# A two-layer kernel (selective scan, then attention): the planner's costs for DMAs, and the queue and the room of the first attention's loads

## The chip, the cores and the metric

The kernel runs on one core of one Trainium2 chip. The metric is the time of one execution on the device, in microseconds. Before the change it is 4532.04 us, the median of three runs (4529.59 to 4533.02).

## The reference

The input `x` is (2, 256, 64, 64) in float32: two images, 256 channels, 4096 positions. Two layers are added to it in turn.

```python
# layer 0: group norm, then a selective-scan block and an MLP
yn = layer_norm(group_norm(x)) * gamma + beta          # over the 256 channels, at each position
xm, z = split(yn @ W_in.T)                              # 512 channels each
u = silu(causal_conv4(xm) + conv_b)
proj = u @ W_xp.T                                       # 16 for dt, 16 for B, 16 for C
dt = softplus(proj[:, :16] @ W_dt.T + b_dt)
h = exp(dt * A) * h + (dt * u) * B                      # for each position, 512 channels x 16 states
y = sum_n(h * C) + u * D
y2 = (y * silu(z)) @ W_out.T + yn
x = x + gelu(y2 @ W1.T + b1) @ W2.T + b2 + y2
# layer 1: group norm, then attention with 8 heads of 32 over the 4096 positions
q, k, v = split(group_norm(x) @ qkv_w.T + qkv_b)
x = x + softmax(q.T @ k / sqrt(32)) @ v.T
```

## The kernel before

Positions are cut into tiles of 512, eight for each image. The kernel has three stages: `mamba_stage` (layer 0 for both images, 16 tiles), then `attention_block` for image 0 and again for image 1. A last check of the softmax sums chooses whether a slow general attention has to run; it does not here.

**The scan.** A tile has 32 steps: four blocks of 128 channels, four groups of four states, two halves. A step multiplies on GpSimd or VectorE (`dbu`, line 809), scans on VectorE (line 814), keeps the last state with a copy on ScalarE (line 817) and multiplies by C on GpSimd (line 820). The decay exponentials are ScalarE's (line 803). The time steps `dt` and `dt * u` go through DRAM so that they can come back replicated over partitions: stores at line 588, loads `dt_rep` and `dtu_rep` at line 767, two of each at the start of a block of channels. Rows of B and C come back the same way (line 779).

**Around it.** `front` prepares the next tile: it loads `yn` (line 481), normalises it (line 479), projects and convolves, and computes `dt`. `back` finishes a tile: the output product, the MLP with eight GELUs into the buffer `hid` (line 646), two long sums over `hid` (line 657), the addition to the loaded `x_back` (line 667), the statistics for the second group norm (line 668) and the store (line 671). From tile 8 on, `qkv` projects one tile of image 0 for the first attention: it loads the weights (line 686) and the tile (line 687) into `hid`, normalises (line 692), makes queries and keys in two halves (lines 705 and 709), stores them (line 714), and does the same for values (lines 741 and 734). `hid` has one buffer, which `back` and `qkv` take in turns.

**The order of work.** None of this is issued as written. Every piece is a task in `Plan`, with an engine, a due step, a cost in microseconds, and for a DMA a time `lands` from its issue being done to its landing. `Plan.order` runs a list schedule in these costs: each engine takes the ready task with the earliest due step, none that is due more than 24 steps behind the oldest open one. A DMA task occupies the planned SP for its cost, and its readers become ready after cost and `lands`. The result is the program order of each engine. On the chip each engine takes its instructions in that order and waits where one is not ready, so a task that was planned too early holds up what stands behind it. All DMAs are issued by SP's queue.

Due steps are written by hand. `qkv(0, t)` is due `QKV` = 20 steps into a tile:

```python
qkv(0, t, (i + 1) * STEPS + QKV)
```

**Room.** Each stage opens pools in on-chip memory, one after the other from the same base, and gives them back at its end. `mamba_stage` has the pool `l0w` (weights and small tables, 51 KB for each partition) and behind it `l0s` (all buffers of the scan, `hid` and `x_back` among them). `attention_block` lays its own pools over the same room, in the order in which they are opened: weights and values (`l1w`: `b_qkv`, `ones`, `v`), queries (`l1p2`), keys (`l1k`), exponentials (`l1e`, `l1c`), and after the loads the result buffers (`l1p1`, `l1p3`) and a key buffer (`l1kq`).

**The attentions.** `attention_block` works on steps of 128 keys by 512 queries for four heads: logits on TensorE (line 1086), exponentials on ScalarE (line 1099), products with the values on TensorE (line 1120), sums on VectorE and GpSimd. For image 0 (`prepared`) queries, keys and values lie in DRAM already, and `load_prepared` brings the first query tile (4 DMAs, line 910), the eight key tiles (2 DMAs each, line 907) and the values (line 1042). For image 1 `prepare` makes them first, which takes about 105 us with the loads at lines 968 and 975.

Of the kernel before, what the change touches and what calls it, by code (L numbers as in the profile page):

```python
# [19 lines left out]
P = 128  # L20
# [81 lines left out]
class Plan:  # L102
# [4 lines left out]

    HANDOVER = 0.2
# [20 lines left out]
    def add(self, engine, due, cost, emit, reads=(), writes=(), tables=(), lands=0.0):  # L129


        task = Plan.Task()
        task.engine, task.due, task.cost, task.emit = engine, due, cost, emit
        task.tables, task.lands, task.at = tables, lands, len(self.tasks)
        deps = set()
        reads, writes = list(self.keys(reads)), list(self.keys(writes))
        for key in reads:
            deps.add(self.writer.get(key))
        for key in writes:
            deps.add(self.writer.get(key))  # L140
            deps.update(self.readers.get(key, ()))
        for key in reads:
            self.readers.setdefault(key, []).append(task)
        for key in writes:
            self.writer[key], self.readers[key] = task, []
        deps -= {None, task}
        task.deps, task.behind = len(deps), []
        task.ready, task.start = 0.0, None
        for dep in deps:
            dep.behind.append(task)  # L150
        task.bufs = list({id(b): b for b, _ in reads + writes}.values())
        for buf in task.bufs:
# [92 lines left out]
QKV = 20  # L245
# [3 lines left out]
def mamba_stage(ctx, tc, xs, stats_out, consts, w, outs, scratch):  # L249
# [220 lines left out]
    def front(i):  # L470
# [10 lines left out]
        add("SP", due - 46, 0.8, lambda: nc.sync.dma_start(yn.tile, image_tile(xs[b], t)), [], [yn], lands=4.0)  # L481
# [58 lines left out]
        add("SP", due - 12, 0.8, store_bc, [bc], [d.bc], lands=2.0)  # L540
# [26 lines left out]
    def softplus(d, k, due):  # L567
# [28 lines left out]
        add("SP", due + 3.5, 0.8, lambda: store(d.dt[k], dt, "dt_dram"), [dt], [d.dt[k]], lands=2.0)  # L596
        add("POOL", due + 3.5, 1.27, lambda: nc.gpsimd.tensor_mul(lw.tile, dt.tile, d.u[k].tile), [dt, d.u[k]], [lw])
        add("SP", due + 4, 0.8, lambda: store(d.dtu[k], lw, "dtu_dram"), [lw], [d.dtu[k]], lands=2.0)
# [12 lines left out]
    def back(i):  # L611
# [26 lines left out]
        add("SP", due + 6, 0.8, lambda: nc.sync.dma_start(xt.tile, image_tile(xs[b], t)), [], [xt], lands=4.0)  # L638
# [33 lines left out]
        add("SP", due + 29, 0.8, store, [xt], [stored[b * NT + t]], lands=3.0)  # L672

    def qkv(b, t, due):
# [19 lines left out]
        add("SP", due, 1.6, load, [stored[b * NT + t]], [hid], lands=6.0)  # L694
        for k in range(KC):
            add("ACT", due + 2, 0.75, lambda k=k: norm(k), [hid[3 + k], scales_buf[(IMAGES + b) * KC + k]], [hid[3 + k]])
        for n, (i, m) in enumerate(((1, 0), (1, 1), (0, 0), (0, 1))):
# [24 lines left out]
            add("SP", at + 1.5, 0.8, store, halves, [], lands=3.0)  # L722
        for j in range(0, T // P, 2):
# [18 lines left out]
            add("SP", at + 1, 1.6, store, [hid[7]], [], lands=3.0)  # L742
# [17 lines left out]
    def load_rep(g, name, src, ring_):  # L760
# [8 lines left out]
        add("SP", g - 7, 0.8, load, [src], [rep], lands=4.5)  # L769
        return rep  # L770

    def load_row(g, ring_, at):
# [8 lines left out]
        add("SP", g - 5, 0.8, load, [tiles[i].bc], [row], lands=4.0)  # L781
# [117 lines left out]
def load_stack(nc, dst, src, which):  # L899

    src = src.rearrange("s c h t -> s c (h t)")
    dst = dst.rearrange("p h t -> p (h t)").bitcast(F32)
    for i in range(2):
        if which:
            nc.sync.dma_start(dst[2 * i * D : 2 * (i + 1) * D, :], src.rearrange("s c x -> (s c) x"))
        else:
            for j in range(2):
                nc.sync.dma_start(dst[(2 * i + j) * D : (2 * i + j + 1) * D, :], src[i])  # L910
# [3 lines left out]
def attention_block(ctx, tc, b, stats, consts, w, out, scratch, range_t, prepared):  # L914
# [15 lines left out]
    wp = ctx.enter_context(tc.tile_pool(name=f"l1w{b}", bufs=1))  # L930
# [3 lines left out]


# [6 lines left out]
    p2 = ctx.enter_context(tc.tile_pool(name=f"l1p2{b}", bufs=2))  # L942
    kp = ctx.enter_context(tc.tile_pool(name=f"l1k{b}", bufs=NT))
    ep = ctx.enter_context(tc.tile_pool(name=f"l1e{b}", bufs=5))
    ec = ctx.enter_context(tc.tile_pool(name=f"l1c{b}", bufs=2))
# [3 lines left out]
    def load_keys(g, t):  # L949
# [3 lines left out]
        load_stack(nc, k, scratch.qk[b * KG + g, 1, t], 1)  # L953

    def load_queries(i):
        if i < KG * NT:
            g, t = divmod(i, NT)
            q = queries[i] = p2.tile([P, 4, T], F32R, name="q")
            load_stack(nc, q, scratch.qk[b * KG + g, 0, t], 0)
# [79 lines left out]
    def load_prepared():  # L1039
        def load_values(g, t):  # L1040
            cs = bass.ts(t, T // P)
            nc.sync.dma_start(v[:, cs, g * P : (g + 1) * P], scratch.v[b * KG + g, :, cs, :])

        with tc.manual_schedule():
            load_queries(0)
            for t in range(NT):
# [195 lines left out]
def attention_any_range(ctx, tc, consts, w, out, scratch):  # L1242
# [20 lines left out]
    with tc.For_i(0, groups, 1) as g:  # L1263
        k = p1.tile([P, NT, 4, T], F32R, name="g_k")
        for t in range(NT):
            load_stack(nc, k[:, t], scratch.qk[bass.ds(g, 1), 1, t].rearrange("o s c h t -> (o s) c h t"), 1)
# [4 lines left out]
        with tc.For_i(0, NT, 1) as t:  # L1271
            q = p1.tile([P, 4, T], F32R, name="g_q")
            load_stack(nc, q, scratch.qk[bass.ds(g, 1), 0, bass.ds(t, 1)].rearrange("o n s c h t -> (o n s) c h t"), 0)
# [120 lines left out]
```

## Time and profile before

| | |
|---|---|
| runs | 4529.59, 4532.04, 4533.02 us |
| profiled execution | 4532.59 us |
| its span, first to last instruction | 4530.8 us |
| scan | 0 to about 2121 us |
| first attention | about 2121 to 3277 us |
| second attention, with its preparation | about 3277 to 4524 us |
| busy over the span: PE, DVE, ACT, POOL | 4248.6, 3931.0, 3762.3, 3821.2 us |
| DMA engines, mean busy share | 28% |

A profile is one execution. Engines are PE (TensorE, with PEld its weight loads), DVE (VectorE), ACT (ScalarE), POOL (GpSimd) and SP, which issues DMAs and is never counted as busy. L820 is line 820 of the kernel. A name such as `h<-h,c` gives what an instruction writes and reads. A wait names the engine and line that ended it. GpSimd and VectorE set the pace of the scan, TensorE that of the attentions (1070.95 us busy of the 1090 us from 2260 on).

### The profile page before, as it was taken

The page shows a single profiled execution, that of the slowest core. Times are in us where ns is not written, and L with a number is a line of the kernel's source. Part 1 is how long each engine was busy: PE and PEld are TensorE (multiplying, and loading weights), DVE is VectorE, ACT ScalarE, POOL GpSimd, SP SyncE. Part 2 cuts the span into 40 slices and gives each one's busy share as a digit, 9 for nine tenths or more (in the row PEclk, how much of TensorE's full clock was granted, in tenths as well). Part 3 has the DMA queues.
Part 4 walks back from the last instruction along what each step waited for, and adds up shares of the span by engine and source line. Part 5 has one row for each costly group of instructions (what it writes and reads, how often), then busy time and mean ns, then how long its engine had stood idle before and what let it go on. Part 6 is the DMA issues. An engine that isn't in the chain of part 4 may idle for free. (4 is left out here: it accounts for less than half of the span.)

```text
span 4530.8 us, 53988 instructions
## 1 busy us (share of the span) xinstructions
PE 4248.6 (94%) x18530; PEld 1638.8 (36%) x18530; DVE 3931.0 (87%) x3316; ACT 3762.3 (83%) x4836; POOL 3821.2 (84%) x2251
## 2 busy tenths in 40 slices
PE   5799989999899999988999999999899999999998
PEld 2233333333333333333333333333343333333333
DVE  4999989999999899994889889898848898898988
ACT  4788888888788888883999999999739999999997
POOL 2999999999999999994888888888708888888887
PEclk8899999999999999999999999999999999999999
DMA  5233333333443344444311040110091100401100
GB/s 191 96 118 114 108 111 121 126 126 126 143 153 124 127 131 135 153 156 106 88 26 26 20 100 17 26 29 20 20 267 40 45 24 22 101 17 26 28 20 8
DMA packets 172938, 389.24 MB, mean 86 GB/s; under 512 B 24048, under 2 KB 50416, under 8 KB 164464
## 3 DMA queue, kind: packets, MB, share of 16 engines
q1 hardware_dynamic: 172656, 385.73, 28.0%
q8 instruction: 147, 2.41, 0.2%
q14 instruction: 135, 1.11, 0.1%
HBM read 292.34 MB, written 93.32 MB: 85 GB/s over the span
## 5 line engine op out<-in xcount | busy, mean ns | idle before, releaser
L1112 DVE TENSOR_REDUCE chunk<-chunk 128x1024 f32<-128x4096 f32 x288 | 1269.9, 4409 | 226.7 <-ACT chunk L1099 226.7
L1099 ACT ACTIVATE chunk<-s 128x1024 f32<-128x1024 f32 x992 | 1116.7, 1126 | 181.2 <-PE s L1086 146.9
L1153 POOL TENSOR_TENSOR acc_p<-acc_p,e 128x1024 f32<-128x1024 f32 x480 | 1153.0, 2402 | 135.2 <-ACT e L1099 114.1
L1086 PE MATMUL s<-q,k 128*128 128x512 f32 x4096 | 1225.6, 421 | 17.5 <-DMA v<-v_dram 14.8
L820 POOL TENSOR_TENSOR h<-h,c 128x1024 f32<-128x1024 f32 x512 | 1206.5, 2368 | 38.4 <-ACT state L817 27.8
L1120 PE MATMUL po<-chunk,v 128*32 128x512 f32 x3968 | 1114.6, 640 | 0.0
L1120 PE MATMUL po<-e,v 128*32 128x512 f32 x4224 | 1079.0, 605 | 0.0
L1099 ACT ACTIVATE e<-s 128x1024 f32<-128x1024 f32 x1056 | 1069.5, 1016 | 7.4 <-PE s L1086 7.0
L1086 PEld LDWEIGHTS s<-q,k 128*128 128x128 f32 x4096 | 689.8, 188 | 1021.5 <-issue 926.4
L803 ACT ACTIVATE da<-dt_rep,neg_a 128x512 f32<-128x512 f32 x1024 | 690.5, 701 | 118.6 <-DVE h L814 87.7
L1151 POOL TENSOR_TENSOR acc_p<-acc_p,e 128x512 f32<-128x512 f32 x480 | 631.2, 1315 | 161.4 <-ACT e L1099 138.6
L814 DVE TENSOR_TENSOR_SCAN h<-da,state,dbu 128x512 f32<-128x512 f32 x512 | 650.3, 1273 | 52.0 <-POOL dbu L809 45.9
L814 DVE TENSOR_TENSOR_SCAN h<-da,state,bn 128x512 f32<-128x512 f32 x512 | 647.4, 1265 | 12.4 <-POOL dt L595 0.5
L809 POOL TENSOR_TENSOR dbu<-dtu_rep,b 128x512 f32<-128x512 f32 x384 | 486.8, 1279 | 30.8 <-DMA dtu_rep<-dtu_dram 27.9
L234 ACT ACT_TABLE_LOAD x338 | 433.7, 1283 | 6.8 <-PEq L1384 0.7
L425 PE MATMUL bn<-proj,pick 112*128 112x512 f32 x512 | 309.2, 617 | 111.3 <-DVE h L814 111.1
L846 PE MATMUL y<-h,sum 128*32 128x512 f32 x2048 | 358.8, 638 | 24.4 <-POOL h L820 24.0
L809 DVE TENSOR_TENSOR bn<-dtu_rep,bn 128x512 f32<-128x512 f32 x512 | 349.1, 682 | 30.6 <-PE bn L425 16.2
L1150 DVE TENSOR_TENSOR acc<-acc,e 128x512 f32<-128x512 f32 x448 | 309.8, 691 | 24.3 <-ACT e L1099 13.8
L1120 PEld LDWEIGHTS po<-chunk,v 128*32 128x32 f32 x3968 | 142.9, 108 | 360.7 <-issue 349.6
L425 PE MATMUL mm<-yn,w_in 128*128 128x512 f32 x512 | 250.4, 615 | 12.3 <-ACT yn L514 9.3
L425 PE MATMUL mm<-xm,taps 128*128 128x512 f32 x512 | 237.1, 606 | 11.1 <-POOL xm L561 8.7
(135 smaller groups left out, 4068.4 us busy)
## 6 DMA issues: line engine op xcount, KB each, us to landing
dt_rep<-dt_dram SPq DMA_DIRECT2D x128, 512.0 KB, 5.0
dtu_rep<-dtu_dram SPq DMA_DIRECT2D x128, 512.0 KB, 5.5
q<-qk_dram SPq DMA_DIRECT2D x128, 256.0 KB, 4.8
k<-qk_dram SPq DMA_DIRECT2D x64, 512.0 KB, 8.1
b<-bc_dram SPq DMA_DIRECT2D x64, 256.0 KB, 3.1
c<-bc_dram SPq DMA_DIRECT2D x64, 256.0 KB, 4.6
dt_dram<-dt SPq DMA_DIRECT2D x64, 256.0 KB, 2.1
dtu_dram<-lw SPq DMA_DIRECT2D x64, 256.0 KB, 3.4
```

The source lines that it names most:

```text
L234: self.nc.scalar.preload_act_table_set(self.TABLES[task.table])
L425: nc.tensor.matmul(out, lhsT=lhsT, rhs=rhs, start=(i == 0), stop=(i == len(pairs) - 1))
L803: nc.scalar.activation(da[j].tile, dt.tile[:, j, :], AF.Exp, scale=scale)
L809: engine.tensor_mul(out.tile, dtu.tile[:, j, :], rows.tile)
L814: nc.vector.tensor_tensor_scan(h.tile[:, j, :], da[j].tile, dbu.tile, initial, ALU.mult, ALU.add)
L820: nc.gpsimd.tensor_tensor(h.tile, h.tile, rows_c.tile.unsqueeze(1).to_broadcast([P, 2, T]), ALU.mult)
L1086: nc.tensor.matmul(ps[:, j, :], lhsT=keys[i // NT, kt][:, h, kj : kj + P], rhs=queries[i][:, h, :], start=True, stop=True)
L1099: nc.scalar.activation(e, todo[s].s[half], AF.Exp, scale=SCALE)
L1112: nc.vector.tensor_reduce(out, terms, AX.XY, ALU.add)
L1120: nc.tensor.matmul(tiles[i].po[h * D : (h + 1) * D, :], lhsT=v[:, c, g * P + h * D : g * P + (h + 1) * D], rhs=todo[s].e[h // 2][:, h % 2, :],
L1151: nc.gpsimd.tensor_add(acc_p[:, 1, :], acc_p[:, 1, :], eb[:, 1, :])
L1153: nc.gpsimd.tensor_add(acc_p, acc_p, eb)
```

## The change

There are two parts.

The planner counts DMAs by their bytes: a load or store of 512 KB holds the planned SP for 1.7 us and lands 3.3 us later, one of 256 KB holds it for about 0.9. In the steps before 32 the cost is at most 0.8. `QKV` goes from 20 to 16. In `qkv` the weights come in two loads of half the size, planned as tasks of their own behind the tile's load.

The first attention's pools are opened in another order, so that exponentials lie over the weights' pool, and queries, result buffers, keys and values over the scan's. Its first query tile, first key tile and first values are issued by ScalarE's queue, as its first instructions behind the scan's; the others stay on SP's.

```diff
     def add(self, engine, due, cost, emit, reads=(), writes=(), tables=(), lands=0.0):
+        if engine == "SP" and due < 32:
+            cost = min(cost, 0.8)
...
-QKV = 20
+QKV = 16
...
-        add("SP", due - 46, 0.8, lambda: nc.sync.dma_start(yn.tile, image_tile(xs[b], t)), [], [yn], lands=4.0)
+        add("SP", due - 46, 1.7, lambda: nc.sync.dma_start(yn.tile, image_tile(xs[b], t)), [], [yn], lands=3.3)
...
-        add("SP", due - 12, 0.8, store_bc, [bc], [d.bc], lands=2.0)
+        add("SP", due - 12, 0.4, store_bc, [bc], [d.bc], lands=1.6)
...
-        add("SP", due + 3.5, 0.8, lambda: store(d.dt[k], dt, "dt_dram"), [dt], [d.dt[k]], lands=2.0)
+        add("SP", due + 3.5, 0.9, lambda: store(d.dt[k], dt, "dt_dram"), [dt], [d.dt[k]], lands=2.0)
...
-        add("SP", due + 6, 0.8, lambda: nc.sync.dma_start(xt.tile, image_tile(xs[b], t)), [], [xt], lands=4.0)
+        add("SP", due + 6, 1.7, lambda: nc.sync.dma_start(xt.tile, image_tile(xs[b], t)), [], [xt], lands=3.3)
...
-        add("SP", due + 29, 0.8, store, [xt], [stored[b * NT + t]], lands=3.0)
+        add("SP", due + 29, 1.7, store, [xt], [stored[b * NT + t]], lands=3.3)
...
+        def load_weights(c):
+            nc.sync.dma_start(weights(c, 0, 3 * C), w["qkv_wT"][c * P : (c + 1) * P, :])
+
         def load():
-            nc.sync.dma_start(flat(0, 3).rearrange("p (k f) -> p k f", k=KC), w["qkv_wT"].rearrange("(k p) f -> p k f", p=P))
             nc.sync.dma_start(hid.tile[:, 3:5, :], image_tile(outs[b], t))
...
-        add("SP", due, 1.6, load, [stored[b * NT + t]], [hid], lands=6.0)
+        add("SP", due, 1.7, load, [stored[b * NT + t]], [hid], lands=3.3)
+        for c in range(KC):
+            w_parts = [hid[0]] if c == 0 else [hid[1], hid[2]]
+            add("SP", due + 1 + c, 1.3, lambda c=c: load_weights(c), [], w_parts, lands=3.0)
...
-            add("SP", at + 1.5, 0.8, store, halves, [], lands=3.0)
+            add("SP", at + 1.5, 1.7, store, halves, [], lands=3.3)
...
-            add("SP", at + 1, 1.6, store, [hid[7]], [], lands=3.0)
+            add("SP", at + 1, 1.0, store, [hid[7]], [], lands=2.5)
...
-        add("SP", g - 7, 0.8, load, [src], [rep], lands=4.5)
+        add("SP", g - 7, 1.7, load, [src], [rep], lands=3.3)
...
-        add("SP", g - 5, 0.8, load, [tiles[i].bc], [row], lands=4.0)
+        add("SP", g - 5, 0.9, load, [tiles[i].bc], [row], lands=3.0)
...
-    wp = ctx.enter_context(tc.tile_pool(name=f"l1w{b}", bufs=1))
+    def pool(name, bufs):
+        return ctx.enter_context(tc.tile_pool(name=f"l1{name}{b}", bufs=bufs))
+
+    def late_pools():
+        return pool("p1", 1), pool("p3", 2)
...
+    ec, ep, p2 = pool("c", 2), pool("e", 5), pool("p2", 2)
+    if prepared:
+        p1, p3 = late_pools()
+    kp, wp = pool("k", NT), pool("w", 1)
...
-    def load_keys(g, t):
+    def load_keys(g, t, queue=nc.sync):
...
-        load_stack(nc, k, scratch.qk[b * KG + g, 1, t], 1)
+        load_stack(queue, k, scratch.qk[b * KG + g, 1, t], 1)
...
         with tc.manual_schedule():
-            load_queries(0)
-            for t in range(NT):
+            load_queries(0, nc.scalar)
+            load_keys(0, 0, nc.scalar)
+            load_values(0, 0, nc.scalar)
+            for t in range(1, NT):
                 load_keys(0, t)
                 load_values(0, t)
...
-    load_prepared() if prepared else prepare()
-
-    p1 = ctx.enter_context(tc.tile_pool(name=f"l1p1{b}", bufs=1))
-    p3 = ctx.enter_context(tc.tile_pool(name=f"l1p3{b}", bufs=2))
-    kq = ctx.enter_context(tc.tile_pool(name=f"l1kq{b}", bufs=1))
+    if prepared:
+        load_prepared()
+    else:
+        prepare()
+        p1, p3 = late_pools()
+    kq = pool("kq", 1)
```

The store of `dtu_dram` changes as that of `dt_dram` does. `load_stack`, `load_queries` and `load_values` take the queue in the same way as `load_keys`.

More of the change, by code (lines that the diff above doesn't have):

```diff
@@ L595, in softplus @@
         add("POOL", due + 3, 1.27, lambda: nc.gpsimd.tensor_add(dt.tile, dt.tile, lw.tile), [lw], [dt])
-        add("SP", due + 3.5, 0.8, lambda: store(d.dt[k], dt, "dt_dram"), [dt], [d.dt[k]], lands=2.0)
+        add("SP", due + 3.5, 0.9, lambda: store(d.dt[k], dt, "dt_dram"), [dt], [d.dt[k]], lands=2.0)
         add("POOL", due + 3.5, 1.27, lambda: nc.gpsimd.tensor_mul(lw.tile, dt.tile, d.u[k].tile), [dt, d.u[k]], [lw])
-        add("SP", due + 4, 0.8, lambda: store(d.dtu[k], lw, "dtu_dram"), [lw], [d.dtu[k]], lands=2.0)
+        add("SP", due + 4, 0.9, lambda: store(d.dtu[k], lw, "dtu_dram"), [lw], [d.dtu[k]], lands=2.0)
     def gate(d, k, due):
@@ L896, in image, with load_stack @@
         return self.x[b * KG : (b + 1) * KG].rearrange("g c t -> (g c) t")
-def load_stack(nc, dst, src, which):
+def load_stack(queue, dst, src, which):
     src = src.rearrange("s c h t -> s c (h t)")
@@ L906, in load_stack @@
         if which:
-            nc.sync.dma_start(dst[2 * i * D : 2 * (i + 1) * D, :], src.rearrange("s c x -> (s c) x"))
+            queue.dma_start(dst[2 * i * D : 2 * (i + 1) * D, :], src.rearrange("s c x -> (s c) x"))
         else:
             for j in range(2):
-                nc.sync.dma_start(dst[(2 * i + j) * D : (2 * i + j + 1) * D, :], src[i])
+                queue.dma_start(dst[(2 * i + j) * D : (2 * i + j + 1) * D, :], src[i])
 @with_exitstack
@@ L941, in attention_block, with load_queries @@
     v = wp.tile([P, NC, C], F32, name="v")
[L942 to L945, printed above, removed]
     keys = {}
     queries = {}
-    def load_keys(g, t):
+    def load_keys(g, t, queue=nc.sync):
         k = keys[g, t] = (kq if g and t == 0 else kp).tile([P, 4, T], F32R, name="k")
-        load_stack(nc, k, scratch.qk[b * KG + g, 1, t], 1)
-    def load_queries(i):
+        load_stack(queue, k, scratch.qk[b * KG + g, 1, t], 1)
+    def load_queries(i, queue=nc.sync):
         if i < KG * NT:
@@ L958, in load_queries @@
             q = queries[i] = p2.tile([P, 4, T], F32R, name="q")
-            load_stack(nc, q, scratch.qk[b * KG + g, 0, t], 0)
+            load_stack(queue, q, scratch.qk[b * KG + g, 0, t], 0)
     def s_tile():
@@ L1039, in load_prepared, with load_values @@
     def load_prepared():
-        def load_values(g, t):
+        def load_values(g, t, queue=nc.sync):
             cs = bass.ts(t, T // P)
-            nc.sync.dma_start(v[:, cs, g * P : (g + 1) * P], scratch.v[b * KG + g, :, cs, :])
+            queue.dma_start(v[:, cs, g * P : (g + 1) * P], scratch.v[b * KG + g, :, cs, :])
         with tc.manual_schedule():
-            load_queries(0)
-            for t in range(NT):
+            load_queries(0, nc.scalar)
+            load_keys(0, 0, nc.scalar)
+            load_values(0, 0, nc.scalar)
+            for t in range(1, NT):
                 load_keys(0, t)
@@ L1265, in attention_any_range @@
         for t in range(NT):
-            load_stack(nc, k[:, t], scratch.qk[bass.ds(g, 1), 1, t].rearrange("o s c h t -> (o s) c h t"), 1)
+            load_stack(nc.sync, k[:, t], scratch.qk[bass.ds(g, 1), 1, t].rearrange("o s c h t -> (o s) c h t"), 1)
         v = p1.tile([P, NC, P], F32, name="g_v")
@@ L1272, in attention_any_range @@
             q = p1.tile([P, 4, T], F32R, name="g_q")
-            load_stack(nc, q, scratch.qk[bass.ds(g, 1), 0, bass.ds(t, 1)].rearrange("o n s c h t -> (o n s) c h t"), 0)
+            load_stack(nc.sync, q, scratch.qk[bass.ds(g, 1), 0, bass.ds(t, 1)].rearrange("o n s c h t -> (o n s) c h t"), 0)
             o = p1.tile([P, T], F32, name="g_o")
```

## The prediction

> **What bounds the kernel now.** I read the page's table of slices first (two even stretches and dips near slices 20 and 30), then busy time by stretch of one scan tile, then the waits of GpSimd and ScalarE in the second half of the scan, the DMA issues, and the timeline where the scan hands over to the first attention. The page's chain of waits ends inside the last 20 us and says nothing of the change.
>
> Busy time in stretches of 123 us (length, then PE, PEld, DVE, ACT, POOL, granted clock, DMA share, GB/s):
>
> ```profile
> 725.00:848.00 123.00, 113.48 (x348) 42.82 (x347) 115.24 (x126) 103.73 (x171) 122.00 (x78) 0.99 0.35 116
> 848.00:971.00 123.00, 114.18 (x347) 43.14 (x346) 115.52 (x127) 103.12 (x171) 122.00 (x80) 0.97 0.35 118
> ...
> 1340.00:1463.00 123.00, 113.93 (x351) 44.43 (x349) 110.92 (x123) 104.00 (x171) 114.43 (x74) 0.97 0.41 135
> 1463.00:1586.00 123.00, 113.14 (x359) 44.71 (x359) 110.23 (x121) 101.07 (x166) 114.16 (x73) 0.99 0.42 140
> ```
>
> In the first image GpSimd works 122.0 of 123 us: nothing is to be won there. In the second, where the projections for the first attention are woven in, it works 114. The last gate product of each tile (line 856 in the timeline) shows the same: tiles 5 to 7 end 120.8 us apart, tiles 8 to 14 end 124.8, 129.4, 128.5, 128.8, 128.1, 126.2 and 125.9 apart. Against 120.8 that is 46 us, the most that a better order could bring. The waits between 1000 and 2090 us (sum, times, longest), first GpSimd's, then ScalarE's:
>
> ```profile
> POOL h L820 <- ACT state L817: 23.3, 25, 3.1
> POOL dbu L809 <- DMA dtu_rep<-dtu_dram: 16.4, 10, 2.5
> ```
>
> ```profile
> ACT hid L705 <- DMA qk_dram<-hid: 24.3, 11, 4.0
> ACT yn L479 <- DMA yn<-in_x: 21.5, 6, 4.9
> ACT da L803 <- DMA dt_rep<-dt_dram: 18.7, 14, 2.8
> ```
>
> The reader is to see two things: GpSimd waits 16.4 us for a transfer itself, and 23.3 us for ScalarE, which in turn sits 64.5 us in its queue before work whose transfer comes later than the planner thought. What transfers take (KB each, median us from issue to landing):
>
> ```profile
> dt_rep<-dt_dram SPq DMA_DIRECT2D x128, 512.0 KB, 5.0
> dtu_rep<-dtu_dram SPq DMA_DIRECT2D x128, 512.0 KB, 5.5
> ...
> qk_dram<-hid SPq DMA_DIRECT2D x32, 512.0 KB, 4.6
> ```
>
> **Part 1, the planner's costs and QKV.** No instruction of the scan is added but one DMA per `qkv` (its weights in two loads instead of one, 8 more issues at 0.39 us each, the row of line 686, on SP, which is idle most of the time: nothing on the path). What changes is the order on each queue. A store of the two halves is now planned to land after 1.7 + 3.3 = 5.0 us, before 0.8 + 3.0 = 3.8, measured 4.6. The four replicated loads that open a block of channels were planned to land at 5.3, 6.1, 6.9 and 7.7 us and are now at 5.0, 6.7, 8.4 and 10.1 (each holds SP 1.7 instead of 0.8); measured 5.0 and 5.5 in the median and up to 9.0. So consumers of late transfers move back in their queues, behind work that is ready. The load of `yn` goes from 4.8 to 5.0, which leaves its 21.5 us. So 24.3 + 18.7 = 43.0 of ScalarE's 64.5 us can go, two thirds; two thirds of GpSimd's 23.3 is 15.5. I take half of that (7.8) and half of the 16.4 (8.2), because a list schedule fills only part of what it now sees: -16. Bounds: all of 16.4 + 23.3, -40; no gain, and a loss through `qkv`, +24, priced under the rivals. Where the stall goes, VectorE is late next: 110 to 112 busy of 123 in those stretches, with 10 us to spare.
>
> The Trainium skill speaks against these costs: "DMA: Bandwidth & Descriptors", section "Anatomy of one DMA — SWDGE (gpsimd) path", fits a transfer as 2.0 us plus its bytes over 436 GB/s, for GpSimd's queue, which for 512 KB makes an estimate of 3.2 us. By it the planner would now be 1.8 us too slow with every such load and part 1 would bring nothing; the rows of 5.0 and 5.5 us on this queue are what I go by.
>
> The start (due below 32) keeps 0.8, with landings 0.7 to 1.2 us earlier than planned before; GpSimd waits 7.4 us there for `dtu_rep`. Either sign, 3 us at most: 0. QKV = 16 raises the rank of the projections by four steps. It does not start them sooner, as `hid` has one buffer: the load at 1320.0 us comes right behind the last matmul that reads `hid`. At the end of the scan it may move one projection (matmuls at 2085.09, 1.88 us) out from between the two output products of the last tile: -1 (0 to -1.9).
>
> **Part 2, the hand-over to the first attention.** The timeline (start, duration, instruction, idle time before):
>
> ```profile
> 2104.36 0.69 ACT L646 ACTIVATE hid<-mm,b 128x512 f32<-128x512 f32 x1 [1.03 <-PE mm L425]
> ...
> 2119.82 0.75 DVE L667 SCALAR_TENSOR_TENSOR x_back<-mm,b,x_back 128x512 f32<-128x512 f32 x1 [6.25 <-PE mm L657]
> ...
> 2120.59 0.37 SPq L671 DMA_DIRECT2D x_dram<-x_back  x1
> ...
> 2120.69 0.12 POOL L940 MEMSET ones<- 128x32 f32 x1 [40.17 <-DVE x_back L667]
> ...
> 2121.53 2.40 SPq L910 DMA_DIRECT2D q<-qk_dram  x4
> 2124.11 1.17 SPq L907 DMA_DIRECT2D k<-qk_dram  x2
> ...
> 2134.61 0.77 PE L1086 MATMUL s<-q,k 128*128 128x512 f32 x1 [14.83 <-DMA v<-v_dram]
> ```
>
> ScalarE is free from 2105.05 us, SP is held by the last store until 2120.59, and TensorE waits 14.83 us for the first loads. If ScalarE's queue could issue at 2105, these would be gone. But look at the memset of `ones`. It is the second small tile of the attention's first pool and lies over the input's statistics, the first tile of the weights' pool, last used long ago. Yet it waits until 2120.6 for the addition that reads `b_2`, the last use of anything in that pool. A new pool's room is free when the whole old pool is. The scan's buffers are one pool too, and `x_back` is in it: its last store is issued at 2120.59 and lands at 2123.45. The waiting instructions of ScalarE, VectorE and GpSimd ahead of their first work over that pool end at 2123.47 to 2123.52, ScalarE's for `chunk`, which lies nowhere near `x_back`. After the change `q`, `k`, `v` lie over the scan's pool alone, so I expect the first load on ScalarE's queue at 2123.5, not 2105, and 2.0 us later than SP's at 2121.53. Its seven issues (2.40 + 1.17 + 0.59 = 4.2 us on SP) hold up only the exponentials, which need their data anyway. The next issues are now on two queues at once: SP follows its small `b_qkv` (3.4 us to land) with the second keys, while ScalarE still has queries and first keys on the way. In the old order q and the first k took 12.7 us from first issue to landing (2121.53 to 2134.20). The DMA engines were 0.89 busy in these 14.8 us with one queue, so a second one only takes turns. From about 2127.5 some 7.2 us of the first loads' transfer time (k lands every 2.4 us) are left; shared in equal turns they take 14.4. So the first matmul comes 2.0 us later with no sharing and 9.2 with full sharing: I take +5, near the middle, since some of SP's loads wait for a landing before they are issued. Low end, if the loads do start at 2105: -13 (rival 1).
>
> On two queues the same page, section "Issuing engines are not separate DMA queues", says that they run on the same 16 engines and that only the issuing time is saved; by it the hand-over would cost the full 9 us, and no run so far has a second queue to show it.
>
> **Part 3, the second hand-over.** The new layout puts the second attention's preparation over the first one's values and not over its result buffers. Its weights' load was issued at 3279.54, once the last result's store (3277.22) had landed at 3279.34; it can now follow the `b_qkv` load, at 3278.1: -1.4 (0 to -1.9). The attentions themselves keep their instructions.
>
> **Sum.** The profiled execution took 4532.59 us (span 4530.8 and 1.8 around it), 0.5 over the median of the runs. 4532.6 - 16 + 5 - 1.4 - 1 = 4519. The forecast's own range is 4496 to 4530.
>
> **Rivals.**
> 1. The loads do start behind the GELU. For it: ScalarE is idle for 30.89 us there. Against: the 40.17 us of `ones`. They would be landed by 2119, the first matmul moves from 2134.61 to 2120.6, and the second keys on SP, issued near 2121.6, cost back about 1: -13 instead of +5, 4501.
> 2. Slower: the `hid` buffer sets the pace. In `qkv` the weights are now planned behind the image's load, since that writes all of `hid`: 5.0 + 1.3 + 1.3 + 3.0 = 10.6 us before the first projection may be planned, 7.6 before. On the chip SP's order follows this. `hid` is held in turn by one projection round and one MLP, a round every 128 us, so 3.0 us in each of 8 rounds would add 24 with no gain to set against: 4532.6 + 24 + 5 - 2.4 = 4559. For it: the first GELU of tile 9 comes 50 us after that tile's end (33 in tile 0). Against: 27 us lie between the last projection (1368) and that GELU, room enough to hide 3. It decides if the time from the load of `qkv` to its first normalisation, 10.1 us now, grows by 3 and the GELUs move with it.
> 3. GpSimd's waits only change their names: its idle time stays near 59.6 us between 1000 and 2090, as VectorE and TensorE (93%) are nearly as full. 4532.6 + 5 - 2.4 = 4535.
>
> **Chances.** Forecast 0.48, rival 1 0.10, rival 2 0.25, rival 3 0.17. A measurement of this kernel tells about 0.2% (9 us) from no change. Faster by more: 0.40 of the forecast and rival 1, 0.50. Within: 0.08 of the forecast and 0.13 of rival 3, 0.21. Slower: rival 2 and the rest of rival 3, 0.29. The range runs from 4494 to 4556: below rival 1's time, and nearly to rival 2's.
>
> **What will show it.** Right: tiles 8 to 14 end near 126 us apart; ScalarE's waits for `qk_dram<-hid` and `dt_rep` halve; the first `q` is issued about 3 us after the last `x_back` addition, and the first matmul of the logits follows 16 to 23 us after that addition (14.0 now). Wrong: a `q` issued before that addition (rival 1), or GpSimd's waits in the second half as large as before under other names.

## The result, and the profile after

The changed kernel takes 4530.25 us in the median of 12 runs (4521.69 to 4533.14), the kernel before 4531.79 beside it (12 runs, 4528.81 to 4536.74). The ratio is 0.9996, with a 95% interval of 0.9988 to 1.0003: no difference that this measurement can tell.

The profiled execution of the changed kernel is the fastest of its twelve (4521.69 us, span 4519.9). Against the profile of before it is 10.9 us shorter, where the medians differ by 1.5. So two profiles alone mislead here, and the phases below are read from several.

First the stall lists, as in the prediction: waits between 1000 and 2070 us (the scan now ends at 2060), sum, times, longest; ScalarE, then GpSimd.

```profile
ACT da L812 <- DVE h L823: 59.9, 59, 2.9
ACT state L826 <- DVE h L823: 52.4, 80, 3.9
ACT hid L714 <- PE mm L429: 20.8, 16, 5.6
ACT da L812 <- DMA dt_rep<-dt_dram: 9.5, 8, 2.6
...
ACT yn L483 <- DMA yn<-in_x: 2.7, 2, 1.9
ACT hid L698 <- DMA hid<-x_dram: 1.6, 2, 1.4
```

```profile
POOL h L829 <- ACT state L826: 17.9, 22, 2.7
POOL dbu L818 <- DMA dtu_rep<-dtu_dram: 7.5, 5, 2.2
```

Beside the first two lines belong two rows of the kernel before (1000 to 2090 us) that the prediction does not show:

```profile
ACT state L817 <- DVE h L814: 42.3, 70, 2.9
ACT da L803 <- DVE h L814: 35.5, 39, 2.9
```

ScalarE's 24.3 us before `hid`, for the store of the last halves, are gone from its list. Its waits for `dt_rep` halve (18.7 before), and those for `yn`, which I had left as they were, are nearly gone (21.5). But ScalarE does not get freer by it: its waits for VectorE's scan grow from 77.8 to 112.3 us, those of `hid` for the projection's matmul from 12.0 to 20.8. Added up over all rows from 1000 to 2060 us, its waits are 177.4 us before and 178.1 after. GpSimd's wait for `dtu_rep` halves (16.4 before). Its wait for ScalarE's state copy, 23.3 before, hardly moves: 17.9 here, 23.5 and 22.7 in the next two profiles with these costs.

Busy time in two of the stretches shown before (length, PE, PEld, DVE, ACT, POOL, granted clock, DMA share, GB/s):

```profile
1340.00:1463.00 123.00, 117.14 (x368) 45.86 (x367) 114.72 (x126) 101.68 (x170) 118.05 (x77) 0.99 0.42 144
1463.00:1586.00 123.00, 116.20 (x365) 45.77 (x364) 114.19 (x127) 106.93 (x177) 118.44 (x76) 1.00 0.45 147
```

GpSimd works 118 of 123 us where it worked 114: here the scan gains. Now what follows it. TensorE from the last product of the scan (`y`) to the last output product (`z,w_out`), the kernel before and then the changed one (start, duration, instruction, idle time before):

```profile
2080.57 1.05 PE L846 MATMUL y<-h,sum 128*32 128x512 f32 x4 [1.44 <-POOL h L820]
2081.55 3.70 PE L621 MATMUL mm<-z,w_out 128*128 128x512 f32 x8
2085.09 1.88 PE L425 MATMUL mm<-hid 128*128 128x512 f32 x4
2086.81 3.60 PE L621 MATMUL mm<-z,w_out 128*128 128x512 f32 x8
```

```profile
2059.42 1.05 PE L855 MATMUL y<-h,sum 128*32 128x512 f32 x4 [2.74 <-POOL h L829]
2060.40 3.71 PE L429 MATMUL mm<-hid 128*128 128x512 f32 x12
2063.95 5.31 PE L625 MATMUL mm<-z,w_out 128*128 128x512 f32 x12
2069.10 1.88 PE L429 MATMUL mm<-hid 128*128 128x512 f32 x4
2070.82 1.88 PE L625 MATMUL mm<-z,w_out 128*128 128x512 f32 x4
2072.53 1.88 PE L429 MATMUL mm<-hid 128*128 128x512 f32 x4
```

The lines with `mm<-hid` are the last projection round. Behind the scan's last product there was one projection (4 matmuls); now there are five (20). The first GELU of the last tile, which writes the same `hid`, starts 10.7 us after the last gate product before (2092.35 against 2081.7) and 19.3 after the change (2079.86 against 2060.52).

And the hand-over to the first attention, from the timeline of the changed kernel:

```profile
2104.94 0.75 DVE L671 SCALAR_TENSOR_TENSOR x_back<-mm,b,x_back 128x512 f32<-128x512 f32 x1 [6.25 <-PE mm L661]
2105.72 0.37 SPq L675 DMA_DIRECT2D x_dram<-x_back  x1
...
2108.66 2.02 ACTq L919 DMA_DIRECT2D q<-qk_dram  x4
...
2108.97 0.12 POOL L960 MEMSET ones<- 128x32 f32 x1 [49.61 <-DMA x_dram<-x_back]
2109.19 4.43 SPq L919 DMA_DIRECT2D q<-qk_dram  x4
2113.63 3.12 ACTq L916 DMA_DIRECT2D k<-qk_dram  x2
...
2130.48 0.77 PE L1107 MATMUL s<-q,k 128*128 128x512 f32 x1 [25.59 <-DMA k<-qk_dram]
```

The last GELU ended at 2090.2, yet the first `q` on ScalarE's queue is issued at 2108.66, 2.97 us after the last addition: all wait for `x_back`'s store. Right behind it stands a thing that nobody asked for: four more `q` on SP's queue, which are the second query tile. Before, that tile was issued at 2180.55, behind all values. The first logits come 24.8 us after the last addition (14.0 before).

### The profile page after: what moved, and what is told of

Same layout as the page of the kernel before. It is cut to its first block, busy times and chain, and to the rows that moved or that the text cites. A ratio compares the mean times of both kernels' runs of the same rounds, so it can differ in the third digit from the quotient of the medians.

```text
span 4519.9 us, 53931 instructions
## 1 busy us (share of the span) xinstructions
PE 4243.8 (94%) x18530; PEld 1639.2 (36%) x18530; DVE 3927.0 (87%) x3316; ACT 3755.3 (83%) x4830; POOL 3821.7 (85%) x2251
## 4 chain that ended last, share of the span: by engine, by line
PE 63%; POOL 12%; DVE 9%; issue 7%; ACT 5%; DMA 3%; SPq 0%; POOLq 0%; DVEq 0%; ACTq 0%
PE s L1107 25%; PE po L1141 24%; PE mm L429 7%; POOL h L829 7%; DVE h L823 6%; POOL dbu L818 3%; ACT da L812 2%; ACT L238 2%; PE y L855 1%; PE mm L661 1%; DVE bn L818 1%; DMA xn<-x_dram 1%; PE mm L625 1%; PE bn L429 1%; POOL lw L598 1%
## 5 line engine op out<-in xcount | busy, mean ns | idle before, releaser
L429 PE MATMUL bn<-proj,pick 112*128 112x512 f32 x512 | 296.7, 596 | 113.4 <-DVE h L823 112.7
L1171 DVE TENSOR_TENSOR acc<-acc,e 128x512 f32<-128x512 f32 x448 | 309.7, 691 | 23.9 <-ACT e L1120 11.3
L429 PE MATMUL mm<-yn,w_in 128*128 128x512 f32 x512 | 253.8, 622 | 10.4 <-ACT yn L518 9.2
L429 PE MATMUL mm<-yn,w 128*128 128x512 f32 x512 | 242.2, 602 | 3.2 <-ACT u L562 1.4
```

The lines of the kernel that those rows point to most:

```text
L429: nc.tensor.matmul(out, lhsT=lhsT, rhs=rhs, start=(i == 0), stop=(i == len(pairs) - 1))
```

## The experiments

The table has one row for each kernel. "Last gate": start of the last gate product; "behind it": from there to the end of the last addition to `x_back`; "logits": from that addition to the first logits. These three come from one profile each. The last two columns are the measured ratio to the kernel before on the same chip, turned into us with that kernel's median there (4528 to 4532 us), and its 95% interval; this differs from the plain difference of the two medians by up to 2.7 us.

```text
kernel            last gate  behind it  logits    difference   interval
before               2081.7       38.9    14.0
b0_before_again      2077.5       38.9    14.1        0.0     -4.5 to  4.5
e4_qkv16             2078.0       38.9    13.7        0.9     -3.6 to  5.0
e9_qkv_costs         2078.6       42.3    14.0        5.0      0.9 to  9.5
e2_handover          2078.6       38.9    24.5        8.1      4.1 to 12.2
e8_replicated        2061.5       46.5    14.1      -10.4    -14.5 to -5.9
e1_planner           2066.3       47.3    14.1       -6.3    -10.4 to -2.3
e3_costs_qkv20       2064.4       46.9    14.3       -2.7     -6.8 to  1.4
after                2060.5       45.2    24.8       -1.8     -5.4 to  1.4
a0_after_again       2066.2       45.2    24.7       -0.5     -5.0 to  3.6
e5_order             2062.3       47.2    21.3        1.4     -2.7 to  5.4
e7_one_queue         2070.3       47.3    15.7       -3.6     -7.7 to  0.5
e6_late_pool         2065.7       49.1     0.1      -20.8    -27.2 to -14.5
e11_best             2062.4       47.9     0.1      -24.5    -30.8 to -18.1
```

**Is the gain in the profile real?** The changed kernel a second time, and the kernel before a second time, both unaltered.

> The changed kernel once more, unaltered, for a second profile. The first profile fell on the fastest of its twelve executions (4521.69 us, their median 4530.25). Theory A (the planner's gain at the end of the scan is real in every execution, the hand-over gives it back): the last gate product again near 2060.5 us (2081.7 before), the first logits again near 24.8 us after the last addition. Rival B (the gain of the scan was that one fast execution): the last gate product between 2068 and 2075 us, with the hand-over unchanged at about 24.8 us and a span near 4528.

> The kernel before once more, unaltered, for a second profile of it: last gate product 2078 to 2082 us, the stretch behind it 38.9 us, first logits 13.7 to 14.1 us after the last addition, second hand-over 116 to 120 us, ratio 1.000. A last gate product at 2070 us or earlier would say that the scan's gain is spread between runs.

The last gate product of the changed kernel fell on 2066.2, between the two bounds; the kernel before had 2077.5, half a microsecond under its forecast. Both theories hold a part. Over the seven kernels with all the new costs it comes at 2065.1 on average (2060.5 to 2070.3), over the four with none of them (before, b0, e4, e2) at 2079.0 (2077.5 to 2081.7). So 13.9 us are the best estimate of the gain; the 21.2 between the first two profiles hold 7 us of spread. At the end of tile 7 the two groups agree, 1070.7 against 1071.0: all of it comes in the second half. The first logits repeat to 0.2 us.

**Which half does what?** The planner's part alone, and the attention's part alone, by joining the one half of the changed kernel to the other half of the kernel before:

```diff
# e1_planner: Plan.add, QKV and the costs in mamba_stage from after; attention_block from before
# e2_handover: mamba_stage and Plan from before; attention_block and load_stack from after
```

> The planner's costs and QKV = 16 alone; the attention as before. Theory A: the whole gain at the end of the scan and none of the hand-over's cost, the last gate product near 2060.5 us, the first logits 14.0 us after the last addition, a time of 4518 to 4521 us. Rival B (the scan's gain is run-to-run spread): 4528 to 4532 us in the median, as the kernel before. If the second hand-over's 6.0 us belong to the new layout alone, the time is 6 us higher than theory A says.

> The planner's costs as before; the attention part of the change alone (loads of queries, keys and values over the scan's buffers, the first ones on ScalarE's queue). Theory A: the first logits about 24.8 us after the last addition instead of 14.0, the scan's end unchanged at 2081.7 us, 4537 to 4543 us (10.75 later, up to 6.0 back in the second hand-over). Rival B: the hand-over costs nothing that the median shows, 4530 to 4533 us.

They gave -6.3 and +8.1: theory A in its signs, though e1's median (4523.3, beside 4527.7 for the kernel before) lies above the 4518 to 4521 of theory A; e2's 4537.7 and its 24.5 us to the first logits lie within it. Both intervals are clear of zero. The sum, +1.8, agrees with the changed kernel's -1.8 and -0.5 within the intervals. That settles the main thing: the change is no null. It is a gain and a loss of one size, in two places.

**Inside the planner's part.** First `QKV`, each way:

```diff
 # e3_costs_qkv20: e1_planner with
-QKV = 16
+QKV = 20
 # e4_qkv16: the kernel before with
-QKV = 20
+QKV = 16
```

> The planner's part alone with QKV left at 20, so only the new costs and the two loads of the projection's weights. Measured for both together: 4523.3 us (4527.7 before), the scan's last gate product 14 to 21 us earlier, but the stretch from it to the last addition 6.3 to 8.4 us longer, as four more projections stand between the last output products. Theory A (the new costs bring the scan's gain, QKV = 16 only moves projections into the last stretch): the last gate product again near 2066 us, the stretch behind it 39 to 41 us instead of 45 to 47, 4516 to 4519 us. Theory D (QKV = 16 brings part of the scan's gain, or the new costs alone put the projections there): the stretch behind it stays at 45 to 47 us, or the last gate product comes 5 us later, 4522 to 4528 us.

> The kernel before with QKV = 16 and nothing else. Theory A: no gain in the scan (last gate product 2079 to 2083 us), the stretch from it to the last addition 43 to 47 us instead of 38.9, a time 4 to 8 us above the kernel before. Theory D: the last gate product 5 us or more earlier, the stretch unchanged, the time equal or less.

Theory A fell in both. With `QKV` at 20 the stretch behind the scan is as long as with 16 (46.9), and with 16 and the old costs it is as short as before (38.9). So `QKV` moves nothing that these runs can tell (the difference between e1 and e3 is 3.6 us, within the intervals); the new costs themselves bring the extra projections behind the scan, as the second half of theory D has it. e3 alone is not clear of zero (-6.8 to 1.4), so the gain of the planner's part rests on e1, on e8 below and on the last gate products. Which of the costs bring it, the next pair tells:

```diff
 # e8_replicated: the kernel before with
+        if engine == "SP" and due < 32:
+            cost = min(cost, 0.8)
...
-        add("SP", g - 7, 0.8, load, [src], [rep], lands=4.5)
+        add("SP", g - 7, 1.7, load, [src], [rep], lands=3.3)
...
-        add("SP", g - 5, 0.8, load, [tiles[i].bc], [row], lands=4.0)
+        add("SP", g - 5, 0.9, load, [tiles[i].bc], [row], lands=3.0)
 # e9_qkv_costs: the kernel before with the new costs and the two weight loads of qkv
...
+            add("SP", due + 1 + c, 1.3, lambda c=c: load_weights(c), [], w_parts, lands=3.0)
...
-            add("SP", at + 1.5, 0.8, store, halves, [], lands=3.0)
+            add("SP", at + 1.5, 1.7, store, halves, [], lands=3.3)
...
```

> The kernel before with only the new costs of the replicated loads (1.7 + 3.3 instead of 0.8 + 4.5) and of the rows b and c (0.9 + 3.0 instead of 0.8 + 4.0), and the old 0.8 at the start. If the gain of the scan comes from these loads: ScalarE's wait for dt_rep and GpSimd's for dtu_rep halve (19 and 16 us before, about 10 and 8 with all costs), the last gate product comes 5 us or more ahead of the 2078 to 2082 us of the kernel before, the wait of hid for qk_dram (24 us) stays, and so does the stretch behind the scan, 38.9 us. If these waits only change their names: the last gate product within 2 us of the kernel before, 4527 to 4530 us.

> The kernel before with only the new costs of the projections for the first attention (store of the halves 1.7 + 3.3 instead of 0.8 + 3.0, the weights in two loads behind the image's). If these make the scan's gain: hid's wait for qk_dram on ScalarE goes from 24 us to 2 at most, the last gate product comes 5 us or more ahead of 2078 to 2082 us, and since the planner now takes a round of projections to be longer, the last round ends behind the scan: the stretch from the last gate product to the last addition grows from 38.9 to 45 us or more. If the other costs make it: no change in the scan, and the stretch stays at 38.9 us.

The costs of the replicated loads and rows by themselves bring the whole gain: -10.4 us, against -6.3 with everything (the intervals overlap). Which of the two brings it, the loads or the rows, no run separates. With e9's +5.0 they make -5.4, so the remaining costs (`yn`, `x_back`, the stores) leave nothing that these runs can tell. Waits of e8, 1000 to 2060 us, GpSimd and then ScalarE:

```profile
POOL h L822 <- ACT state L819: 18.9, 24, 1.8
...
POOL dbu L811 <- DMA dtu_rep<-dtu_dram: 7.7, 5, 2.1
```

```profile
ACT da L805 <- DMA dt_rep<-dt_dram: 14.8, 12, 2.4
ACT hid L707 <- DMA qk_dram<-hid: 14.8, 9, 3.6
...
ACT yn L481 <- DMA yn<-in_x: 0.9, 2, 0.5
```

and e9's, GpSimd and then ScalarE:

```profile
POOL h L825 <- ACT state L822: 33.7, 33, 3.0
POOL dbu L814 <- DMA dtu_rep<-dtu_dram: 12.7, 10, 2.4
```

```profile
ACT hid L694 <- DMA hid<-x_dram: 14.9, 5, 6.4
ACT da L808 <- DMA dt_rep<-dt_dram: 8.1, 7, 2.2
ACT yn L479 <- DMA yn<-in_x: 7.6, 3, 3.7
...
ACT hid L710 <- DMA qk_dram<-hid: 2.8, 2, 2.2
```

e9 takes 19 to 25 us of waits for the store of the halves off ScalarE, and some 11 of those for `dt_rep` (all in these 1060 us of before and b0), and is 5.0 us slower. In return the normalisation of the projection's image, which waited 0.6 to 1.8 us for its load before, waits 14.9. e8 leaves more than half of the `dt_rep` and `hid` waits where they were (it was expected to halve the first and leave the second alone), halves GpSimd's own wait for `dtu_rep`, and gains. All of ScalarE's waits for transfers together fall by the same in both, from 64.6 and 67.7 us (before, b0) to 34.5 in e9 and 33.3 in e8, and only e8 gains: these waits were not what held the scan. What tells the two apart stands in GpSimd's rows: `dtu_rep` 7.7 us in e8, 12.7 in e9 (16.4 and 13.3 in before and b0), and the wait for the state 18.9 in e8, 33.7 in e9 (19.8 and 22.8). GpSimd's idle time in these 1060 us says the same: 56.4, 51.7 and 55.9 us in before, b0 and e4, and 57.6 in e9; 43.3, 43.5, 45.7 and 44.4 in after, e1, e3 and e8.

e8 also has the long stretch behind the scan (46.5, where 38.9 was expected), though no cost in `qkv` is changed; in e9 it is 42.3. My reading: the projections keep a pace of their own, bound to the one buffer `hid`, and a scan that ends earlier leaves more of their last round behind it. It fits all rows of the table (the kernels with a late last gate have 38.9 to 42.3, those with an early one 45.2 to 49.1), and the traces fit it: in all fourteen the last round's first load is issued 0.1 us behind the last matmul that reads `hid`, and on average this comes 8.2 us earlier with all the new costs, where the last gate product comes 13.9 earlier. But the planner's order also places these projections, and no run changed the number of `hid` buffers: the cause of the longer stretch is argued, not shown.

**Inside the hand-over.** Three suspects: the room (all loads wait for `x_back`'s store), the second queue, and the second query tile that jumped ahead. It could jump because the loads and the attention's work stand in two separate hand-ordered blocks: in one block (e5, e7) it stays behind. The kernel before has the two blocks too, and there it did not jump; what in the change let it go ahead, no run separates. e5 puts the loads inside the main block; e7 does so and has all on SP's queue; e6 keeps e5's queues and takes away what the loads wait for.

```diff
 # e5_order: after with
-        with tc.manual_schedule():
-            load_queries(0, nc.scalar)
...
     with tc.manual_schedule():
+        if prepared:
+            load_prepared()
 # e7_one_queue: e5_order with
-        load_queries(0, nc.scalar)
-        load_keys(0, 0, nc.scalar)
-        load_values(0, 0, nc.scalar)
+        load_queries(0)
+        load_keys(0, 0)
+        load_values(0, 0)
```

> The changed kernel with the first attention's loads issued inside the same hand-ordered block as the attention's own work, so that the second tile of queries stays behind the keys and values on SyncE's queue. Theory A (the second queries' four loads at 2109.19 us take the landing signals and the engines' turns from the first keys): first logits 16 to 20 us after the last addition instead of 24.8, 4522 to 4526 us in the median. Rival C (two queues that share the engines are the cost, whatever their order): first logits still 23 to 25 us after it, 4530 us.

> The changed kernel with the loads in one hand-ordered block and all of them on SyncE's queue, over the scan's buffers as in the change: only the room differs from the kernel before. Theory A (the wait for the store's landing costs 2 to 3 us, the second queue the rest): first logits 16 to 18 us after the last addition (21.3 with the first loads on ScalarE's queue, 24.8 in the changed kernel), 4524 to 4527 us. Rival (the late room alone sets it, because all loads start at once behind one landing): 20 us or more.

The profiles give the price of each suspect. Issue and landing of the first attention's first loads, in us after the last addition, worked out from the traces:

```text
                  before (SP)     e7 (SP)         e5 (ACT)        after (ACT)
first of q0       0.96   5.16     3.50   6.74     2.97   7.11     2.97   7.60
last of q0        2.95   8.82     5.00  10.46     4.81  13.52     4.56  15.58
first of k0       3.54  11.21     5.46  12.90     5.30  17.37     7.94  19.96
second of k0      4.12  13.63     6.04  15.27     5.86  20.70    10.58  24.66
first logits          14.04           15.71           21.27           24.80
```

The room costs 1.7 us (15.71 against 14.04), the second queue 5.6 (21.27), the second query tile in front 3.5 (24.80); together the 10.8. e7's 15.7 and its median of 4526.1 us are what its theory A said (16 to 18, 4524 to 4527), to 0.3 us. The matmul starts 0.1 to 0.6 us behind the landing of the second half of `k0` in each. e5's 21.3 lies between theory A's 16 to 20 and rival C's 23 to 25: both were right in part, the second queue with the larger share. In the last columns of the table e5 is no better than the changed kernel (1.4 against -1.8 and -0.5), which the intervals, 4 us either way, allow; the 3.5 us are read from the traces alone.

How the second queue delays the first load can be read in e5's timeline. SP, which has only the small `b_qkv` to issue before, starts on the second key tile at 2113.01, ahead of the first key tile on ScalarE's queue (2114.82):

```profile
2112.49 2.30 ACTq L919 DMA_DIRECT2D q<-qk_dram  x4
2114.82 1.17 ACTq L916 DMA_DIRECT2D k<-qk_dram  x2
```

```profile
2113.01 4.14 SPq L916 DMA_DIRECT2D k<-qk_dram  x2
```

A `k` half landed every 2.4 us on one queue (11.21, 13.63; 12.90, 15.27); on two, the halves of the second tile landed at 11.06 and 19.33, one ahead of both halves of the first and one between them (17.37, 20.70). The Trainium skill says in "DMA: Bandwidth & Descriptors", section "Issuing engines are not separate DMA queues", that transfers of all issuing engines interleave on the same 16 engines and that a second one saves only issuing time; e5 against e7 agrees: the four `q` and four halves of `k` have landed by 20.70 us in e5 and by 21.18 in e7, which has one `v` more by then. It also shows that the second queue isn't neutral: what is needed first gives turns to what is needed later.

**Without the wait.** e6 also gives `yn`, `hid` and `x_back` a pool of their own between the weights' and the scan's, and lays the attention's queries, keys and values past it:

```diff
 # e6_late_pool: e5_order with
+    lt = ctx.enter_context(tc.tile_pool(name="l0t", bufs=2))
     sb = ctx.enter_context(tc.tile_pool(name="l0s", bufs=2))
...
-    r_yn, r_u, r_z = ring("yn", 3, KC), ring("u", KD + 1), ring("z", KD)
+    r_yn, r_u, r_z = ring("yn", 3, KC, pool=lt), ring("u", KD + 1), ring("z", KD)
...
-    r_hid, r_xb = ring("hid", 1, KH), ring("x_back", 1, KC)
+    r_hid, r_xb = ring("hid", 1, KH, pool=lt), ring("x_back", 1, KC, pool=lt)
...
-    ec, ep, p2 = pool("c", 2), pool("e", 5), pool("p2", 2)
+    ec, ep = pool("c", 2), pool("e", 5)
     if prepared:
         p1, p3 = late_pools()
+        kq = pool("kq", 1)
+    p2 = pool("p2", 2)
```

> The changed kernel, with the loads inside the same hand-ordered block and the buffers that the last tile still uses (yn, hid, x_back) in a pool of their own, over which no load of queries, keys or values of the first attention lies. The first loads no longer wait for the landing of x_back's last store. If that wait, and the loads' 15 to 25 us behind it, are the whole cost of the first hand-over: the first q is issued on ScalarE's queue within 2 us after the last GELU, some 13 us ahead of the last addition, and the first logits come 0 to 5 us after that addition (24.8 in the changed kernel, 14.0 before), 4506 to 4512 us in the median. If something else holds the first loads or the first logits (the landing signals, ScalarE's own queue, the data of the projections), the logits stay 14 us or more behind the addition and the time stays at 4522 us or more.

It came out at 4507.2 us in the median of 5 runs, by the measured ratio 20.8 us below the kernel before. From its timeline, ScalarE's queue and then TensorE (the last addition ends at 2114.78):

```profile
2078.96 0.40 ACTq L920 DMA_DIRECT2D q<-qk_dram  x1
...
2098.57 0.69 ACT L651 ACTIVATE hid<-mm,b 128x512 f32<-128x512 f32 x1 [1.03 <-PE mm L430]
2098.58 1.39 ACTq L917 DMA_DIRECT2D k<-qk_dram  x2
```

```profile
2111.68 2.31 PE L662 MATMUL mm<-hid,w 128*128 128x512 f32 x5
2114.83 1.67 PE L1106 MATMUL s<-q,k 128*128 128x512 f32 x6 [0.84 <-DVE x_back L672]
```

The four queries go out from 2078.96 us on, the first of them 20.3 us ahead of the last GELU's end and not behind it as expected; the first keys are issued as that GELU starts, and the first logits start 0.06 us after the last addition. With the same order and the same queues, but over the scan's one pool, it was 21.3 (e5): the wait for the room was the cost. All loads on SP's queue over this room were not tried, so what the second queue adds here stays open.

**The two gains together.** e8's costs with e6's hand-over:

> The two parts that gained, together: of the planner's part only the new costs of the replicated loads and rows (measured alone: 10.4 us less), of the hand-over the loads in one hand-ordered block over room that does not hold yn, hid and x_back (with the whole planner's part: 20.8 us less, of which the planner's part alone gave 6.3, so 14.5 for the hand-over). If the two add up: 24 to 26 us below the kernel before, first logits within 1 us of the last addition. If the earlier scan and the early loads get in each other's way (the last round of projections and the loads on one SyncE queue): no better than 20.8 us below it.

4505.0 us, by the ratio 24.5 below the kernel before, where the two by themselves make 24.9 (10.4 and 14.5): they add up as far as can be told, for the interval (18.1 to 30.8) holds e6's 20.8 too. This is the lowest median of all, 0.54% faster (0.40 to 0.68) than the kernel before, with the first logits 0.05 us after the last addition.

## Why the prediction was right or wrong

The predicted range held the time, but the forecast did not come true: 13 us were to be gained, and 1.5 were. The sum was off above all in two terms, both in one direction. Of its signs, the tiles (8 to 14 end 125.0 us apart on average, 127.4 before), ScalarE's waits for `qk_dram<-hid` and `dt_rep` and the issue of the first `q` came as said; the first matmul of the logits, at 24.8 us instead of 16 to 23, did not.

- **Part 1, -16 for the scan.** Nearly the size measured: the last gate product came 13.9 us earlier. The way to it was half wrong. Of the terms, 8.2 for GpSimd's wait for `dtu_rep` is what came (16.4 to 7.5); the 7.8 by way of ScalarE's waits did not (the wait for the state was 20 to 24 us before and 18 to 24 with all the new costs). That the sum still came near was in part luck: where the other 6 us come from, no run shows. The step that failed is from ScalarE's waits for transfers to GpSimd's: they fall from 64.6 to 13.8 us (1000 to 2060 us), and ScalarE waits for VectorE's scan instead (70.7 us, then 112.3). Taking off ScalarE's 24.3 us before `hid`, more than half of the 43 us that this step counted on, gained nothing, and the edits that do it cost 5.0 by themselves (e9). And "the load of `yn` goes from 4.8 to 5.0, which leaves its 21.5 us" was wrong: it went to 2.7, and to 0.9 in e8, where no cost of `yn` changed. The replicated loads stand beside it in SP's order: before, two `dtu_rep` and the rows went out in the 2.6 us ahead of it and it landed 5.9 to 8.0 us after its issue (five loads from 1311 to 1826 us); in e8 one `dtu_rep` stands 0.6 to 0.9 us ahead and it lands after 5.5 to 7.0. I had looked at each DMA's own landing, not at what the others do to its place.
- **The tail, -1.** The mis-sized term of part 1: it is +8.0 (46.9 against 38.9 on average). I asked what the change of `QKV` does to the last round, when `QKV` does nothing measurable (e4: 0.9, -3.6 to 5.0), and never asked where that round would stand if the scan ended 16 us sooner. I had the sentence that the load of the image comes right behind the last reader of `hid`, and did not ask what follows from it here. -13.9 + 8.0 is -5.9; e1 measured -6.3.
- **Part 2, +5.** The step that the loads wait for `x_back`'s store was right to the tenth (2.97 us after the last addition, 3 predicted), and so was the pool as its reason (e6). The size was too small, +10.6 on average of three profiles, above even the 9.2 that I gave for full sharing. What failed: I let SP follow with "the second keys", in the order of the source. The second query tile came first, 1 MB that I had not counted. Without it (e5) the delay is 7.2 us, inside my bounds of 2.0 to 9.2. In e5 SP does go on with the second keys, and the turns they take are 5.6 of the 7.2.
- **Part 3, -1.4.** The first projection of the second attention's preparation starts 22.9 us after the first attention's last logits in the seven kernels with the new layout, 23.9 in the seven without: -1.0. The weights' load is issued 0.87 us behind the last result's store instead of 2.32, as predicted. The whole gap from the first attention's last logits to the second's first, 119.8 us before and 113.8 after in the first two profiles, spreads from 113.8 to 119.0 with the new layout and from 115.1 to 121.8 without: those 6.0 us are mostly spread.
- **Together**, -13.9 + 8.0 + 10.6 - 1.0 make +3.7, where the changed kernel measured -1.8 (-5.4 to 1.4) and -0.5 (-5.0 to 3.6). Some 4 us of the terms are not accounted for; each is read from one profile of each kernel.
- **Rival 1** was refused for the right reason, and its price was right: with the room moved the first logits come 0.06 us after the last addition instead of 14.1, and e6 against e1 is 14.5 us, where I worked out 13.
- **Rival 2** named the right place with the wrong size and the wrong signature. The `qkv` costs alone cost 5.0 us (0.9 to 9.5), not 24. The time from the image's load to its first normalisation did not grow: 8.0 us in the median of the eight rounds before, 5.6 after. But the whole round did, from its first load to the end of its last projection: 41.8 and 41.4 us in the median in before and b0, 45.3 and 45.5 in after and a0, 46.0 in e9, and 41.5 in e8, without these costs. So rounds are some 4 us longer, and the time is not eight times that: the `hid` buffer did not set the pace of the whole second half.
- **Rival 3**, waits that only change their names, holds for ScalarE (177.4 and 178.1 us in sum) and not for GpSimd, whose idle time fell by some 11 us.

Two numbers in the text were misread. The first GELU of tile 9 starts at 1376.4 us, 8.4 behind the 1368 that the text starts from, and not 27; the GELU at 1395.3 is a later one. The 27 spoke against rival 2 and changes none of the terms. And 0.39 us is the shortest issue of a weights' load; the median is 0.53, and nothing rests on it.

## What to carry to other kernels

Price a change at the end of a stage together with what runs beside it: here a scan that ended 13.9 us sooner left a stretch behind it that was 8.0 us longer. A wait that ends is not a gain until the engine that sets the pace is shown to idle less. When loads are to start early, look first for the last user of anything in the room they will lie in, and move that room before the queue. A second issuing queue is not free: here its later transfers took turns from the first ones; holding them back until those have landed was not tried. Program order across blocks is not to be assumed, but read from the list of issues.

## What the runs showed of the hardware

- The same program differs in its scan from execution to execution: the last gate product lay at 2060.5 and 2066.2 us in two profiles of the changed kernel, at 2081.7 and 2077.5 in two of the kernel before, and twelve runs of the changed kernel spread over 11.5 us. The granted clock does not tell them apart (0.975 in the profiles of after and of a0, which are 9.6 us apart in span).
- No more than eight transfers were ever under way in the hand-over, on one queue or on two (counted in the traces of before, after, a0, e2, e5 and e7). In the changed kernel seven query loads and `b_qkv` were the eight: the first half of `k0` was issued at 7.94 us after the addition, `b_qkv` had landed at 7.92; the second half at 10.58, a query had landed at 10.56. So here loads in front held up the issue of later ones too.
- `b_qkv`, 3 KB, took 2.1 us from issue to landing where the queries were issued behind it on the same queue (e7), and 4.8 where they went out beside it on the other (after).
